# Queues of bulk transfers, split set-up work, and reordered norms in a kernel of two cross-attention layers

## The chip, the cores and the metric

The kernel runs on one core of one Trainium2 chip. The metric is the device time of one execution in microseconds (us), here the median of three runs. A core has a matrix engine, TensorE (PE in the profile, with its weight loads as PEld), and three engines for element-wise work: VectorE (DVE), ScalarE (ACT) and GpSimd (POOL). SyncE (SP) issues transfers between memory and the core; ACT can issue them too, in order with its own computations. Every engine works through its own instructions in order and waits for the others by semaphores.

## The reference

2048 tokens of width 512 (32 sequences of 64) pass through four blocks, each with a residual. `ctx` has the same shape and is the source of keys and values. Masks and shapes apart:

```
x = x + attention0(layernorm(x), ctx, ctx, mask)   # 32 query heads, 8 key heads, rope on q and k
x = x + ffn(layernorm(x))       # silu(h Wg) * (h Wu), then Wd; 4-bit weights, unpacked as
                                # sc[g_idx] * (nibble - (zero[g_idx] + 1))
x = x + attention1(layernorm(x), ctx, mask)        # RMS norm on q and k, with weights
h = layernorm(x);  x = x + h + gate(h) * aux(h)    # aux: 8 slots chosen of 128, softmax over them
```

and the last block, cut to what the change touches:

```
def _L1_ffn_ref(hidden_states, ...):
    ...
    top_scores, top_idx = jax.lax.top_k(router_scores, K)
    ...
    w = jax.nn.softmax(attn, axis=-1)        # over the 8 slots chosen of 128
    sel_vals = aux_values[top_idx]
    aux_out = jnp.einsum('bsk,bskh->bsh', w, sel_vals)
    aux_out = aux_out @ Wvd.T @ Wvu.T
    ...
    gate = jax.nn.sigmoid(gate_w1 * u_norm + gate_bias)
    gate = jnp.where(gate < EARLY_EXIT, 0.0, gate)
    return hidden_states + gate[..., None] * aux_out
```

## The kernel before

The tokens stand in four chunks of 512 (`c` = 0 to 3); `x_sb[c]`, the transposed normalised `xnT[c]` and the transposed `ctxT[c]` stay in on-chip memory throughout. `norm_stats` takes mean and variance on DVE and the inverse root on POOL; `norm_apply` normalises four tiles on DVE (`xna`, `xnb`, `xnc`, `xnd` for the four norms, L167), transposes them on PE (`xta` to `xtd`, L172) and copies them with ACT into `xnT` (L175).

Attention runs over 8 key heads `g` times 4 chunks `c`, 32 steps. `project` makes the four query heads of a group (`pq`), keys and values (`pv`, or `pkv` in layer 1), with the rope on DVE and its last addition on POOL (`qT`, `kT`, L299); in layer 1 `kn` and `pk` are the normalised keys. `scores` makes `S`, `softmax` the probabilities `s`, `values` the product `po` and, by ACT copies, `oT` (L476), and `output` adds `pout` to `x_sb` (L486, L493). In `Attention.run` the order by hand is: the hooks of the step, loads of the next group, values of the step before, scores, output of the step before, softmax, and projection of the next step. A scheduler orders what is free to move by the data it needs; the order within an engine is fixed when the program is built.

The feed-forward block runs over 6 groups of 256 inner columns times 4 chunks: `ffn_load` fetches the 4-bit weights, `ffn_dequant` unpacks them with DVE, using products of PE (`pgz`, `pdz`) of the one-hot group index `oh` with scales and zero points `sz`; `ffn_up` makes `pgu`, `ffn_down` `pd`. `sz` and `oh` are made once by `ffn_constants`: six scale pieces for gate and up and one for down (`scales_gu`, `scales_down`), two zero-point pieces (`qz`, unpacked into `zi`), and four group-index pieces (`g_idx_gu`, `g_idx_down`), each fetched into a temporary tile, of which there are two, shared with the rope. The whole function is the hook of step (1,0).

The last block: `mem_constants` loads and folds its weights (hook of layer 1's step (1,0)); per chunk `mem_weights` makes router scores and takes the best 8, `mem_softmax` is a softmax over 128 slots for each of four token tiles, `mem_values` transposes the weights (`pwt`, copied to `wT`) and multiplies with the folded values (`paux`), `mem_gate` makes the gates, and `mem_out` adds and stores.

Transfers before: on SP's queue the weights of each group and `x` of chunks 1 to 3; on ACT's queue the first `x`, `ctxT`, `cosT`, `sinT`, the masks (`mraw`, `mask0`), the norm weights `q_norm` and `k_norm`, and all of `ffn_constants` and `mem_constants`.

Of the kernel before, what the change touches and what calls it, by code (L numbers as in the profile page):

```python
# [18 lines left out]
P = 128  # L19
# [23 lines left out]
def tile_xattn_ffn_2_layers(ctx: ExitStack, tc: tile.TileContext, a: dict, out: bass.AP):  # L43
# [19 lines left out]
    def m2_tile(name):  # L63
        return ap_.tile([P, CH], F32, tag="m2", name=name, bufs=4)
# [55 lines left out]
    def load_mask(c):  # L120
        w = NH * KH * S
        mraw[c] = m2_tile(f"mraw{c}")
        nc.scalar.dma_start(mraw[c][:, 0:w], a["mask1"][:, c * w : (c + 1) * w])

    def mask_flags(c):
        w = NH * KH * S
# [72 lines left out]
    class Attention:  # L199
# [31 lines left out]

        def load_out(self, g):
            w = w8_tile(f"wo{self.L}_{g}")
            nc.sync.dma_start(
                w,
                a[self.names[3]][g * GQ * HD : (g + 1) * GQ * HD, :].rearrange(
                    "(h p) n -> p h n", p=P
                ),
            )
            self.wo[g] = w  # L240

        def project(self, g, c):
            return self.project0(g, c) if self.L == 0 else self.project1(g, c)
# [251 lines left out]
        def start(self):  # L495
            self.state = self.project(0, 0)

        def run(self, hooks, joined, after, between=lambda c: None):

            steps = [(g, c) for g in range(NKV) for c in range(NCH)]
            state = self.state
            before = None
            for i, (g, c) in enumerate(steps):
                for hook in hooks.get((g, c), ()):
                    hook()
                if c == 0 and g + 1 < NKV:
                    self.load_in(g + 1)
                if c == NCH - 1 and g + 1 < NKV:  # L510
                    self.load_out(g + 1)
                if before is not None:
                    oT = self.values(*before)
                st, rb = self.scores(g, c, state)
                if g == NKV - 1 and c > 1:
                    between(c - 2)
                if before is not None:
                    self.output(*before[:2], oT)
                probs = self.softmax(g, c, st, rb)
                done = before is not None and before[0] == NKV - 1  # L520
                if done:
                    joined(before[1])
                if i + 1 < len(steps):
                    nxt = self.project(*steps[i + 1])
                if done:
                    after(before[1])
                before, state = (g, c, state, probs), nxt
            oT = self.values(*before)
            between(NCH - 2)
            self.output(*before[:2], oT)  # L530
            joined(before[1])
# [5 lines left out]
    ffn = {}  # L537

    def ffn_constants():

        sz = const.tile([P, 2 * INTER], BF16, tag="sz", name="sz")
        oh = const.tile([P, INTER], BF16, tag="oh", name="oh")
# [16 lines left out]
        for base, cnt, name in ((R_GS, NG, "scales_gu"), (R_DS, NGD, "scales_down")):  # L559
# [3 lines left out]
            for at in range(0, total, CH):  # L563
                w = min(CH, total - at)
                s = tmp_tile(f"{name}{at}")
                v, part = s[rows, 0, 0:w], s[:, 1, :].bitcast(BF16)[rows, 0:w]
                for k in range(3):
                    nc.scalar.dma_start(
                        s[base + k * cnt : base + (k + 1) * cnt, 0, 0:w], a[name][:, at : at + w]
                    )  # L570
                for by in (p1, p2):
                    nc.vector.tensor_copy(part, v)
                    nc.vector.scalar_tensor_tensor(v, part, by, v, ALU.mult, ALU.add)
                nc.vector.tensor_copy(sz[rows, at : at + w], v)
        qz = m2_tile("qz").bitcast(U32)
        zi = m2_tile("zi").bitcast(U32)
        for base, cnt, name in ((R_GZ, NG, "qzeros_gu"), (R_DZ, NGD, "qzeros_down")):
            w = a[name].shape[1]
            rows = slice(base, base + cnt)
            nc.scalar.dma_start(qz[rows, 0:w], a[name])  # L580
            zv = sz[rows, 0 : 8 * w].rearrange("p (w e) -> p w e", e=8)
            for e in range(8):
                nc.vector.tensor_scalar(
# [5 lines left out]
                    ALU.bitwise_and,  # L589
                )  # L590
                nc.vector.tensor_copy(zv[:, :, e], zi[rows, 0:w])
        for base, cnt, parts, name in (
            (R_GS, NG, 3, "g_idx_gu"),
            (R_GZ, NG, 1, "g_idx_gu"),
# [5 lines left out]
            for at in range(0, total, CH):  # L600
                w = min(CH, total - at)
                gt = tmp_tile(f"{name}{base}_{at}")
                gv, o = gt[rows, 0, 0:w].bitcast(I32), gt[rows, 1, 0:w]
                nc.scalar.dma_start(
                    gv, a[name][0:1, at : at + w].to_broadcast([parts * cnt, w])
                )

# [3 lines left out]
                nc.vector.tensor_scalar(  # L611
                    oh[rows, at : at + w], o, pidx[rows, 0:1], None, ALU.is_equal
                )
        ffn["sz"], ffn["oh"] = sz, oh

    groups = [(f, min(FG, INTER - f)) for f in range(0, INTER, FG)]
# [86 lines left out]
    def ffn_down(i, c, hT):  # L703
        tiles = ffn_tiles(i)
        for tk in range(TT):
# [8 lines left out]
                )  # L714
            nc.vector.tensor_tensor(x_sb[c][:, tk, :], x_sb[c][:, tk, :], p, ALU.add)

    def ffn_run(hooks, joined, last):


# [6 lines left out]
                joined(pending[1])  # L726

        for i, c in steps:
            hT = ffn_up(i, c)
            for hook in hooks.get((i, c), ()):  # L730
                hook()
            if pending is not None:
# [9 lines left out]

    mem = {}

    def mem_constants():
        fc = const.tile([P, KT * (BOT + P) + D + 3 * NSLOT + 5], F32, tag="fc", name="fc")
        tp = a8_tile("memtmp").rearrange("p a b -> p (a b)")
        at = [0, 0]
# [4 lines left out]
            at[which] += width  # L753
            return s

        q = nc.scalar
        mem["wq"] = carve(0, P, KT * BOT).rearrange("p (k n) -> p k n", k=KT)
        mem["wu1"] = carve(0, P, KT * P).rearrange("p (k n) -> p k n", k=KT)
        mem["v3"] = carve(0, P, D)
# [12 lines left out]
        q.dma_start(mem["wq"], a["WqT"].rearrange("(k p) n -> p k n", p=P))  # L772
        q.dma_start(mem["wu1"], a["Wu1T"].rearrange("(k p) n -> p k n", p=P))
        q.dma_start(mem["lr"], a["log_rel"].to_broadcast([P, NSLOT]))
        q.dma_start(mem["wu2"], a["Wu2T"])
        q.dma_start(mem["bu1"], a["bu1"])
        q.dma_start(mem["gw"], a["gate_w1"].to_broadcast([P, 1]))
        q.dma_start(mem["gb"], a["gate_bias"].to_broadcast([P, 1]))
        q.dma_start(mem["bu2"], a["bu2"].to_broadcast([P, 1]))
        q.dma_start(keys, a["keysT"])  # L780
        q.dma_start(wr, a["Wr"])
        q.dma_start(wrT, a["WrT"])
        q.dma_start(valT, a["valuesT"].rearrange("(k p) n -> p k n", p=P))
        q.dma_start(wvd, a["WvdT"].rearrange("(k p) n -> p k n", p=P))
        q.dma_start(wvu, a["WvuT"])

        p = mm_tile("prk")
        nc.tensor.matmul(p[0:RDIM, 0:NSLOT], wrT, keys, start=True, stop=True)
# [14 lines left out]
        nc.vector.tensor_copy(mem["v3"], p)  # L803
        mem["vst"] = const.tile([P, NT, 2], F32, tag="vst", name="vst")
        mem["lrn"] = const.tile([P, NT], F32, tag="lrn", name="lrn")

    def mem_each(c, t, xn):

# [55 lines left out]
    def mem_softmax(c, behind=None):  # L864
        if behind is not None:
            with tc.issue_after(behind):
                return mem_softmax(c)
        att, bc = mem["att", c], [P, TT, NSLOT]
        mx = sm.tile([P, TT], F32, tag="mx", name=f"mmx{c}")
        sums = sm.tile([P, TT], F32, tag="sums", name=f"msum{c}")  # L870
# [76 lines left out]
    att0, att1 = Attention(0), Attention(1)  # L947
    last = NCH - 1
    att0.load_kv(0)
    att0.load_q(0)  # L950
    load_ctx(0, nc.scalar)
    nc.scalar.dma_start(cosT, a["cosT"])
    nc.scalar.dma_start(sinT, a["sinT"])
    load_mask(0)
    for c in range(1, NCH):
        load_x(c, nc.sync)
        load_ctx(c, nc.scalar)
        if c == 1:
            att0.load_out(0)
    for j in range(4):  # L960
        nc.scalar.dma_start(mask0[j * KB : (j + 1) * KB], a["mask0"])
# [7 lines left out]
    def behind_first(c):  # L969
        with tc.issue_after(first):  # L970
# [120 lines left out]
```

## Time and profile before

| | |
|---|---|
| three runs | 3195.83, 3197.95, 3198.1 us; median 3197.95 |
| profiled execution | 3197.32 us; its span 3195.5 us, mean granted clock 0.98 |
| idle before the first transpose of PE | 11.9 us |
| largest waits of PE after that | 15.5 (`pq`), 9.7 (`pwt`), 7.6 (`pk`) us |
| PE's time in `pout`, `pq` of layer 0, `pq` of layer 1 | 901.0, 447.0, 451.1 us |
| one step of layer 0's attention | about 38.5 us |
| moved bytes | 67.13 MB, mean 21 GB/s |

The granted clock is the share of full speed at which PE was allowed to run. Times within the execution count from the start of its span. A wait is written as: who waited, for which tile, then who released it.

### The profile page before, as it was taken

How to read it: one execution, taken by the hardware profiler on the slowest of the kernel's cores; microseconds unless marked ns; L12 is line 12 of the kernel's file. 1: busy time of each engine (PE TensorE's matmuls, PEld its weight loads, DVE VectorE, ACT ScalarE, POOL GpSimd, SP SyncE). 2: the span in 40 equal slices, each digit the busy share in tenths (PEclk: the TensorE clock that was granted, in tenths of full speed). 3: DMA queues.
4: the chain of work that ended last, by engine and by line, in shares of the span. 5: the costliest groups of instructions: out<-in, count | busy, mean ns of one | idle time of the engine just before them, and what ended most of it. 6: DMA issues, size and time to landing. Idle time of an engine off the chain costs nothing. (4 is left out here: it accounts for less than half of the span.)

```text
span 3195.5 us, 30089 instructions
## 1 busy us (share of the span) xinstructions
PE 3094.4 (97%) x12454; PEld 1590.4 (50%) x12454; DVE 1466.0 (46%) x2384; ACT 503.7 (16%) x917; POOL 609.1 (19%) x464
## 2 busy tenths in 40 slices
PE   6999999999999999999999999999999999999987
PEld 3545555555555555444444455555555555555443
DVE  6586555554555556323222443343443433333455
ACT  0100000001101001100000122222222222222222
POOL 2212222222222222000000022222222222222221
PEclk8999999999999999999999999999999999999998
DMA  5010101010000000000000000000000000100001
GB/s 173 5 36 1 34 1 34 0 34 19 15 20 14 20 14 20 13 20 20 5 20 16 20 7 26 14 20 14 20 14 20 14 25 10 33 1 14 1 1 53
DMA packets 54159, 67.13 MB, mean 21 GB/s; under 512 B 6229, under 2 KB 29901, under 8 KB 54023
## 3 DMA queue, kind: packets, MB, share of 16 engines
q1 hardware_dynamic: 46284, 57.75, 5.5%
q10 hardware_dynamic: 7739, 7.47, 0.7%
q8 instruction: 98, 1.61, 0.2%
q14 instruction: 38, 0.31, 0.0%
HBM read 61.01 MB, written 4.19 MB: 20 GB/s over the span
## 5 line engine op out<-in xcount | busy, mean ns | idle before, releaser
L486 PE MATMUL pout<-wo,oT 128*128 128x512 f32 x2048 | 901.0, 598 | 6.9 <-ACT oT L476 6.9
L486 PEld LDWEIGHTS pout<-wo,oT 128*128 128x128 f32 x2048 | 385.5, 191 | 496.0 <-issue 462.3
L276 PE MATMUL pq<-xnT,wq 128*128 128x512 f32 x1024 | 447.0, 595 | 15.5 <-ACT xnT L175 15.5
L340 PE MATMUL pq<-xnT,wq 128*128 128x512 f32 x1024 | 451.1, 593 | 0.0
L276 PEld LDWEIGHTS pq<-xnT,wq 128*128 128x128 f32 x1024 | 195.3, 191 | 261.5 <-issue 245.1
L691 PE MATMUL pgu<-xnT,wgu 128*128 128x512 f32 (+1 forms) x704 | 315.4, 606 | 0.3 <-DVE wgu L649 0.2
L340 PEld LDWEIGHTS pq<-xnT,wq 128*128 128x128 f32 x1024 | 192.6, 191 | 216.6 <-issue 214.7
L449 POOL TENSOR_TENSOR s<-s,ib 128x512 f32<-128x512 f32 x128 | 160.6, 1276 | 677.8 <-DVE ib L190 669.3
L493 DVE TENSOR_TENSOR x<-x,pout 128x512 f32<-128x512 f32 x256 | 169.3, 670 | 140.6 <-PE pout L486 140.5
L316 PE MATMUL pkv<-wkv,ctxT 128*128 128x256 f32 x1024 | 226.6, 379 | 0.4 <-DVE x L493 0.4
L691 PEld LDWEIGHTS pgu<-xnT,wgu 128*128 128x128 f32 (+1 forms) x704 | 134.9, 192 | 177.4 <-issue 171.4
L316 PEld LDWEIGHTS pkv<-wkv,ctxT 128*128 128x128 f32 x1024 | 194.6, 190 | 40.3 <-issue 13.8
L299 POOL TENSOR_TENSOR qT<-rope 128x512 f32<-128x512 f32 x128 | 162.1, 1267 | 263.9 <-DVE rope L298 260.6
L296 DVE TENSOR_TENSOR rope<-pq,cosT 128x512 f32<-128x512 f32 x160 | 110.5, 691 | 222.1 <-PE pq L276 141.3
L145 POOL TENSOR_TENSOR qr<-qs,nhalf 128x16 f32<-128x16 f32 x32 | 92.8, 2901 | 446.8 <-DVE qs L375 446.8
L356 DVE TRANSPOSE_TENSOR_REDUCE part<-q 128x16 f32<-128x512 f32 x128 | 90.7, 708 | 174.2 <-ACT q L353 169.9
L263 ACT COPY v<-pv 128x512 f32<-128x512 f32 x32 | 18.8, 588 | 872.3 <-PE pv L256 838.8
L708 PE MATMUL pd<-wd,hT 128*128 128x512 f32 (+1 forms) x352 | 155.0, 592 | 0.0
L476 ACT COPY oT<-po 128x512 f32<-128x512 f32 x256 | 131.7, 599 | 104.4 <-PE po L468 99.9
L468 PE MATMUL po<-s,v 32*128 32x256 f32 x2048 | 140.6, 396 | 5.3 <-DVE rope L298 4.3
L444 ACT ACTIVATE s<-s 128x1024 f32<-128x1024 f32 x64 | 67.6, 1057 | 473.1 <-DVE s L442 473.1
L700 DVE TENSOR_TENSOR hT<-hT,pgu 128x512 f32<-128x512 f32 (+1 forms) x44 | 30.2, 687 | 240.9 <-PE pgu L691 240.9
(205 smaller groups left out, 2631.4 us busy)
## 6 DMA issues: line engine op xcount, KB each, us to landing
wq<-in_L_wq SPq DMA_DIRECT2D x8, 1024.0 KB
wo<-in_L_wo SPq DMA_DIRECT2D x8, 1024.0 KB
wq<-in_L_wqT SPq DMA_DIRECT2D x8, 1024.0 KB
wo<-in_L_woT SPq DMA_DIRECT2D x8, 1024.0 KB
wgu<-in_qweight_gu SPq DMA_DIRECT2D x40, 128.0 KB
ctxT<-in_ctxT ACTq DMA_DIRECT2D x4, 1024.0 KB
out<-o SPq DMA_DIRECT2D x16, 256.0 KB
x<-in_x SPq DMA_DIRECT2D x12, 256.0 KB
```

The costliest lines, as they stand in the source:

```text
L276: nc.tensor.matmul(ps, lhsT, rhs, start=(k == 0), stop=(k == KT - 1))
L296: nc.vector.tensor_tensor(t3[:, 0], ps3, over(cosT, 0, HD), ALU.mult)
L299: nc.gpsimd.tensor_tensor(dst, t3[:, 0], t3[:, 1], ALU.add)
L316: nc.tensor.matmul(ps[:, t], ctxT[c][:, k, tok : tok + P], wkv[:, k], start=(k == 0), stop=(k == KT - 1),)
L340: nc.tensor.matmul(ps, wq[:, k, j * HD : (j + 1) * HD], xnT[c][:, k, :], start=(k == 0), stop=(k == KT - 1),)
L449: nc.gpsimd.tensor_tensor(sv[:, f], sv[:, f], ib[:, f * W : (f + 1) * W].unsqueeze(1).to_broadcast([P, KH, W]), ALU.mult,)
L468: nc.tensor.matmul(po[j][:, f * W : (f + 1) * W], v[rows, f, e], probs[rows, f, e], start=(e == 0), stop=(e == KH - 1),)
L476: ins = nc.scalar.copy(o5[:, j], po[j].rearrange("p (f h q) -> p f h q", f=NH, h=GQ))
L486: nc.tensor.matmul(ps, oT[:, h, t * P : (t + 1) * P], self.wo[g][:, h, :], start=(h == 0), stop=(h == GQ - 1),)
L493: nc.vector.tensor_tensor(x_sb[c][:, t, :], x_sb[c][:, t, :], ps, ALU.add)
L691: nc.tensor.matmul(p[0:w_, :], w[:, k, j, t * P : t * P + w_], xnT[c][:, k, :], start=(k == 0), stop=(k == KT - 1),)
L708: nc.tensor.matmul(p, hT[0:w_, t, tk * P : (tk + 1) * P], wd[i][0:w_, t, :], start=(t == 0), stop=(t == len(tiles) - 1),)
```

## The change

Five things change.

The transfers of `ctxT`, `cosT`, `sinT`, the masks, the norm weights, the feed-forward constants and the last block's constants are issued by SP; ACT issues the first `x` alone. Their order at the start becomes: keys and values, `ctx` 0, queries, `cos`, `sin`, mask 0, `x` 1, `ctx` 1, output weight, then `x` and `ctx` of chunks 2 and 3, `mask0`, norm weights.

`ffn_constants` becomes a generator of 13 pieces, and each step of the groups 1 to 6 runs the next one, until there are none.

The first `ffn_up` is placed behind the last projection of layer 0's attention (`tail`), ahead of that attention's last `norm_apply` calls; the last chunk's norm moves from the hook of (0,0) to that of (0,1); and layer 1's first projection is placed ahead of the norm of chunk 2.

`mem_constants` is placed behind the load of an output weight of layer 1.

`mem_softmax` takes the negated maximum as the bias of one exponential for each token tile, whose running sum is kept (`mem["sums"]`); the weights are no longer divided by their sum, and `mem_out` divides the gate by it.

```diff
-        nc.scalar.dma_start(mraw[c][:, 0:w], a["mask1"][:, c * w : (c + 1) * w])
+        nc.sync.dma_start(mraw[c][:, 0:w], a["mask1"][:, c * w : (c + 1) * w])
...
-            nc.sync.dma_start(
+            ins = nc.sync.dma_start(
...
             self.wo[g] = w
+            self.loaded = ins.ins
...
                     nxt = self.project(*steps[i + 1])
+                else:
+                    tail()
...
                 for k in range(3):
-                    nc.scalar.dma_start(
+                    nc.sync.dma_start(
...
                 nc.vector.tensor_copy(sz[rows, at : at + w], v)
+                yield
...
-            nc.scalar.dma_start(qz[rows, 0:w], a[name])
+            nc.sync.dma_start(qz[rows, 0:w], a[name])
...
                 nc.vector.tensor_copy(zv[:, :, e], zi[rows, 0:w])
+            yield
...
-                nc.scalar.dma_start(
+                nc.sync.dma_start(
                     gv, a[name][0:1, at : at + w].to_broadcast([parts * cnt, w])
...
+            yield
         ffn["sz"], ffn["oh"] = sz, oh
...
+    def ffn_first():
+        ffn["first"] = ffn_up(0, 0)
...
-            hT = ffn_up(i, c)
+            hT = ffn_up(i, c) if (i, c) != (0, 0) else ffn["first"]
...
-    def mem_constants():
+    def mem_constants(behind):
...
-        q = nc.scalar
+        q = nc.sync
...
+        with tc.issue_after(behind):
+            q.dma_start(mem["wq"], a["WqT"].rearrange("(k p) n -> p k n", p=P))
...
         nc.vector.tensor_reduce(mx, att, AX.X, ALU.max)
-        nc.vector.tensor_tensor(att, att, mx.unsqueeze(2).to_broadcast(bc), ALU.subtract)
-        nc.scalar.activation(att, att, AF.Exp)
-        nc.vector.tensor_reduce(sums, att, AX.X, ALU.add)
-        nc.vector.reciprocal(sums, sums)
-        nc.vector.tensor_tensor(att, att, sums.unsqueeze(2).to_broadcast(bc), ALU.mult)
+        nc.vector.tensor_scalar(mx, mx, -1.0, None, ALU.mult)
+        for t in range(TT):
+            nc.scalar.activation(
+                att[:, t, :], att[:, t, :], AF.Exp, bias=mx[:, t : t + 1],
+                accum_out=mem["sums"][:, c * TT + t : c * TT + t + 1],
+            )
...
         gate = mem["gate", name]
+        sums = mem["sums"][:, c0 * TT : c1 * TT]
+        nc.vector.reciprocal(sums, sums)
+        nc.vector.tensor_tensor(gate, gate, sums, ALU.mult)
...
     att0.load_kv(0)
+    load_ctx(0, nc.sync)
     att0.load_q(0)
-    load_ctx(0, nc.scalar)
-    nc.scalar.dma_start(cosT, a["cosT"])
-    nc.scalar.dma_start(sinT, a["sinT"])
+    nc.sync.dma_start(cosT, a["cosT"])
+    nc.sync.dma_start(sinT, a["sinT"])
     load_mask(0)
-    for c in range(1, NCH):
+    load_x(1, nc.sync)
+    load_ctx(1, nc.sync)
+    att0.load_out(0)
+    for c in range(2, NCH):
         load_x(c, nc.sync)
-        load_ctx(c, nc.scalar)
-        if c == 1:
-            att0.load_out(0)
+        load_ctx(c, nc.sync)
     for j in range(4):
-        nc.scalar.dma_start(mask0[j * KB : (j + 1) * KB], a["mask0"])
-    nc.scalar.dma_start(wqk[:, 0:1], a["q_norm"])
-    nc.scalar.dma_start(wqk[:, 1:2], a["k_norm"])
+        nc.sync.dma_start(mask0[j * KB : (j + 1) * KB], a["mask0"])
+    nc.sync.dma_start(wqk[:, 0:1], a["q_norm"])
+    nc.sync.dma_start(wqk[:, 1:2], a["k_norm"])
...
+    pieces = ffn_constants()
...
-            (1, 0): [ffn_constants],
+            **{
+                (g, c): [lambda: next(pieces, None)] for g in range(1, NKV - 1) for c in range(NCH)
+            },
...
+        tail=ffn_first,
...
-            (0, 0): [lambda: norm_apply(last, "b")],
+            (0, 1): [lambda: norm_apply(last, "b")],
...
-        lambda: (norm_apply(last - 1, "c"), att1.start()),
+        lambda: (att1.start(), norm_apply(last - 1, "c")),
...
-        {(0, 1): [lambda: norm_apply(last, "c")], (1, 0): [mem_constants]},
+        {(0, 1): [lambda: norm_apply(last, "c")], (1, 0): [lambda: mem_constants(att1.loaded)]},
```

In the built program the pieces end up thus on DVE: a scale piece stands between the last rope and the predicated copy of its step; both zero-point pieces stand together ahead of the ropes of step (2,3); the sixteen small operations of `pidx` (L555 to L558) stand ahead of the first `xna`, where seven of them stood behind the third.

More of the change, by code (lines that the diff above doesn't have):

```diff
@@ L496, in start, with run @@
             self.state = self.project(0, 0)
-        def run(self, hooks, joined, after, between=lambda c: None):
+        def run(self, hooks, joined, after, between=lambda c: None, tail=lambda: None):
             steps = [(g, c) for g in range(NKV) for c in range(NCH)]
@@ L771, in mem_constants @@
         v2 = carve(1, VB, NSLOT)
[L772 to L785, printed above, removed]
+        with tc.issue_after(behind):
+            q.dma_start(mem["wq"], a["WqT"].rearrange("(k p) n -> p k n", p=P))
+            q.dma_start(mem["wu1"], a["Wu1T"].rearrange("(k p) n -> p k n", p=P))
+            q.dma_start(mem["lr"], a["log_rel"].to_broadcast([P, NSLOT]))
+            q.dma_start(mem["wu2"], a["Wu2T"])
+            q.dma_start(mem["bu1"], a["bu1"])
+            q.dma_start(mem["gw"], a["gate_w1"].to_broadcast([P, 1]))
+            q.dma_start(mem["gb"], a["gate_bias"].to_broadcast([P, 1]))
+            q.dma_start(mem["bu2"], a["bu2"].to_broadcast([P, 1]))
+            q.dma_start(keys, a["keysT"])
+            q.dma_start(wr, a["Wr"])
+            q.dma_start(wrT, a["WrT"])
+            q.dma_start(valT, a["valuesT"].rearrange("(k p) n -> p k n", p=P))
+            q.dma_start(wvd, a["WvdT"].rearrange("(k p) n -> p k n", p=P))
+            q.dma_start(wvu, a["WvuT"])
         p = mm_tile("prk")
@@ L805, in mem_constants @@
         mem["lrn"] = const.tile([P, NT], F32, tag="lrn", name="lrn")
+        mem["sums"] = const.tile([P, NT], F32, tag="msums", name="msums")
     def mem_each(c, t, xn):
@@ L867, in mem_softmax @@
                 return mem_softmax(c)
-        att, bc = mem["att", c], [P, TT, NSLOT]
+        att = mem["att", c]
         mx = sm.tile([P, TT], F32, tag="mx", name=f"mmx{c}")
-        sums = sm.tile([P, TT], F32, tag="sums", name=f"msum{c}")
         nc.vector.tensor_reduce(mx, att, AX.X, ALU.max)
-        nc.vector.tensor_tensor(att, att, mx.unsqueeze(2).to_broadcast(bc), ALU.subtract)
-        nc.scalar.activation(att, att, AF.Exp)
-        nc.vector.tensor_reduce(sums, att, AX.X, ALU.add)
-        nc.vector.reciprocal(sums, sums)
-        nc.vector.tensor_tensor(att, att, sums.unsqueeze(2).to_broadcast(bc), ALU.mult)
+        nc.vector.tensor_scalar(mx, mx, -1.0, None, ALU.mult)
[4 more added lines that the diff above has]
+            )
     def mem_values(c):
```

## The prediction

> **What bounds the kernel now.** I read the engines' shares first, then TensorE's waits, then the timeline around each wait, and last the windows for the clock. The shares and the slices:
>
> ```profile
> PE 3094.4 (97%) x12454; PEld 1590.4 (50%) x12454; DVE 1466.0 (46%) x2384; ACT 503.7 (16%) x917; POOL 609.1 (19%) x464
> PE   6999999999999999999999999999999999999987
> ```
>
> TensorE (PE) is the bound from the second slice on, and the change takes no matmul away. So it can win only PE's idle time, 3195.5 - 3094.4 = 101.1 us, and busy time spent at a lowered clock. Any cost on DVE, ACT, POOL or a queue counts only if PE waits for it. PE's waits (who waited <- who released: sum, times, longest):
>
> ```profile
> PE pq L276 <- ACT xnT L175: 15.5, 1, 15.5
> PE pout L486 <- ACT oT L476: 6.9, 4, 3.3
> PE xtc L172 <- DVE xnc L167: 4.9, 1, 4.9
> PE po L468 <- DVE rope L298: 4.3, 3, 1.9
> PE xtb L172 <- DVE xnb L167: 3.8, 1, 3.8
> ```
>
> The two largest waits besides, 11.9 us before the first transpose and 9.7 us before the last `pwt`, sit at the start and the end. The timeline tells why the first wait above exists (start, duration, engine or issue queue, count, idle time before and its releaser):
>
> ```profile
> 23.63 7.90 ACTq L961 DMA_DIRECT2D mask<-in_mask  x4
> 34.38 1.28 ACT L175 ACT_TABLE_LOAD   x1 [34.38 <-DMA mask<-in_mask]
> 37.78 2.93 PE L276 MATMUL pq<-xnT,wq 128*128 128x512 f32 x3 [15.48 <-ACT xnT L175]
> ```
>
> ACT's own queue was issuing transfers until 34.38 and only then copied `xnT`, although the transposes were there at about 14. Windows (busy of PE, PEld, DVE, ACT, POOL, then PE's granted clock, DMA share, GB/s):
>
> ```profile
> 24.00:26.00 2.00, 0.00 (x0) 0.00 (x0) 1.51 (x4) 0.00 (x0) 0.00 (x0) 0.79 1.04 385
> 42.00:54.00 12.00, 12.00 (x30) 5.29 (x29) 6.38 (x10) 0.00 (x0) 4.73 (x4) 0.99 0.00 0
> 250.00:262.00 12.00, 10.10 (x30) 5.74 (x29) 10.37 (x15) 1.66 (x3) 6.00 (x5) 0.57 0.00 0
> 480.00:560.00 80.00, 80.00 (x344) 40.95 (x343) 41.20 (x60) 7.39 (x12) 18.89 (x15) 1.00 0.10 34
> ```
>
> The reader is to see that transfers run at 385 GB/s early on, that a stall also halves the clock for a time after (0.57 around 256; the clock falls in multiples of 3.41 us), and that in the steady part PE is full while DVE idles half of the time.
>
> **The start.** The mask and norm-weight loads, `ctx`, `cos`, `sin` and mask pieces leave ACT's queue; ACT keeps the first `x` and then copies. The wait of 15.48 goes. PE's granted clock was 0.5 from 25.1 to 42.2; of that, 4.2 us of busy time would have taken 2.1. Against it, sixteen small `pidx` operations now all stand before the first `xna` on DVE, where seven stood after the third: at some 0.15-0.17 us each (`DVE L556 TENSOR_SCALAR pidx` took 0.15) that makes 2.65 us later for the first transpose, all of it exposed. The last `pq` group ends at 53.80 - 15.48 - 2.1 + 2.65 = 38.9, a gain of 14.9. Does SP's single queue keep up? Ahead of `pq` stand `wk`, `wv`, `ctx0`, `wq0` beside `x0`: 3.7 MB; the first 10 us moved 2.8 MB (282 GB/s), the rest at 385 GB/s is there at 12.3, and `pq` wants it at 25. `x2`, whose statistics stand between two ropes on DVE, is there after 8.3 MB, at 24.3, and the rope behind it is wanted at 28.5. So nothing waits, with 4 us to spare at the tightest place.
> What is late next: S(0,0) needs the last rope and its POOL addition, 3.8 us behind the last `pq` (57.56 - 53.80). Before, PE filled 2.8 us of that with sixteen transposes and one first product. After, `xna` of chunk 1 stands behind that rope on DVE and only one transpose group (0.5) fits: 2.3 us lost. Such a pause (3.3 us) is the size of the one that ended at 208.79 (3.26 us), after which the clock was 0.5 for 3.41 us, 1.7 us of work: I take 1.6. Start: 14.9 - 2.3 - 1.6 = **11.0** (9 to 13). The 0.91 us gap before `po` at 82.22 (released by a rope of DVE, which has chunk 2's statistics behind it by then) I count as gone: **0.9** (0 to 0.9).
>
> **Constants in pieces.** Before, one hook at step (1,0) put all 13 groups into the queues: their issues stood on ACT's queue and their conversions on DVE. Between 202 and 255 PE paused 1.41, 3.26, 0.82, 1.52 and 1.90 us, 8.9 in all:
>
> ```profile
> 249.53 2.94 PE L468 MATMUL po<-s,v 32*128 32x256 f32 x8 [1.52 <-DVE rope L298]
> 254.38 2.08 PE L468 MATMUL po<-s,v 32*128 32x256 f32 x8 [1.90 <-DVE rope L298]
> ```
>
> and ran at half clock for 3.4 us from 209.5 and 10.2 us from 250.4, busy 3.4 and 8.3 of them: 11.7 x 1/2 = 5.9. Here a rule and the row part. The Trainium skill, "TensorE: Matmul & The Clock Gate" (section "Why this matters for your kernels"), says that the clock falls after an idle pause of more than about 3 us between bursts. By it only the 3.26 us pause costs clock, the pauses of 0.8 to 1.9 us cost none, and the stretch is worth 8.9 + 1.7 = 10.6. The row shows 0.57 in a window whose longest pause is 1.90, so I count 8.9 + 5.9 = 14.8.
> In the changed kernel a scale piece is five DVE operations (0.41 + 0.73 + 0.41 + 0.73 + 0.40 = 2.7 us) in a step that has 38.5 us, of which DVE is busy 41.2 / 80 = half; it stands between the last rope and the predicated copy, where DVE idles 5.2 us in every step. Hidden. The two zero-point groups did not separate: their 32 operations (8 x (0.33 + 0.95 + 0.19 + 0.31) = 14.2 us, some 17 with the gaps) stand together ahead of the ropes of step (2,3), as they stood before ahead of those of (1,0), where S paused 1.41. That pause I keep, with 0.9 of its kind behind it. Each later `g_idx` piece of twelve operations is 6 us, 1 to 3 over its cover, but the probabilities are ready some 23 us before `po` wants them. So 14.8 - 2.3 = **12.5**; ends 9 (the rule) and 14.8.
> SP's queue: a piece's DMA waits in order behind a weight load that waits for its buffer. A load of 1 MB takes 2.7 us at 385 GB/s and is wanted about three steps (115 us) later. Cost 0. If the cover is gone, the piece stands in front of DVE's next ropes: see the third rival.
>
> **Norms behind first products.** At the end of layer 0 the wait of 3.76 before `xtb` gets 13.9 us of first `pgu` products ahead of it: 3.76, and the clock window at 0.5 from 1298.3 (3.41, busy) 1.7: **5.5** (3.8 to 6). The half clock from 1264.2 to 1281.2 comes from dequantisation among S and `pgz`, which no edit moves: 0. Before the second attention the wait of 4.94 before `xtc` gets `pkv` and `pq` ahead (14 us): 4.94, and of the 0.5 window from 1806.9 (6.8 us, busy 3.7) 1.8: **6.7** (5 to 7). The 7.61 pause before `pk` waits for `kn`, whose copies stand behind an exponential on ACT; it stays, ends -3 to +3.
>
> **Slot sums from the exponential.** Per chunk DVE loses a subtraction (0.69), a reduction (0.68), a reciprocal (0.18) and a product (0.87), 2.4 us, and gains a negation (0.16). ACT's one exponential over 512 columns (0.63) becomes four over 128 with a sum. From rows: an exponential over 12 columns took 0.21, so one over 128 is 0.21 + 116 x 0.42/500 = 0.31, four 1.2. The skill, "ScalarE: Activation LUTs" (section "Rules for kernel authors"), speaks against the split: about 0.3 us for every ACTIVATE and 0.83 ns a column, thus 4 x 0.41 = 1.6 against 0.73. By row ACT loses 0.6, by rule 0.9; the sum's own cost shows in no row (0 to 0.2 each). DVE's chain is 2.2 shorter against it, so the chain wins 1.0 to 1.6 at each use. In the last steps the two pauses of 1.6 before `paux` shorten to about 0.7, the one of 0.39 goes and that of 3.22 shortens by about 1: **3.0**. At the end DVE runs without a break from 3170 to 3192: less 2.4, plus 0.16, plus two reciprocals and products on small tiles (4 x about 0.2) is 1.4; the output transfers, 4.2 MB from 3180.17 on, need 10.9 of the 11.9 us in which they are issued, so I take **1.3**. The 14 loads of the last layer's constants on SP are wanted over 1000 us later or once at `prk`: 0.
>
> **The sum.** 11.0 + 0.9 + 12.5 + 5.5 + 6.7 + 4.3 = 40.9 us. The profiled execution took 3197.32 (span 3195.5); 3197.3 - 40.9 = 3156.4. The median of the runs shown is 0.6 above the profiled one, so 3157.
>
> **Rivals.**
> 1. *The pauses move instead of going.* The zero points stall PE as 248-256 shows, clock included, and the start waits for `x2` or `mask` behind the 1 MB loads on the one queue. The stretch is then worth 3 and the start 6: 40.9 - 9.5 - 5.0 = 26.4, 3171. For it: 32 DVE operations in one lump, and PE idle after the first heads. Against: 4 us to spare.
> 2. *The clock gives more.* With pauses gone, half-clock windows that I left (17 us from 1264, 6.8 from 1858, 10.2 from 3114, 13.6 from 3175) shrink by half: 24 us at half, up to 12 more and so 3145. Against: their pauses remain.
> 3. *Slower: DVE waits in line for a piece.* Its conversion cannot be passed; behind it are the next ropes, behind these S. DVE can lose about 5.2 us before the copy and 8 before a rope stops PE (17 us of zero points made 1.41), 13 in all. If SP holds back pieces behind a weight load that waits for its buffer, one whole step each (38.5) in the three groups, PE stops 25.5 us times 3 for two pieces each, 153 us: 3197 - 41 + 153 = 3309. It decides, slower than before, from a sum of 41 us past the cover, 3.2 us per piece. Against: the buffer that `wq` waits for comes free within the step before.
> 4. *The table of waits names the wrong releaser at the start*, and `xnT` is late for another reason: without the start 3168, and 3180 if the constants' stretch too is set by DVE work that is all still there.
>
> Chances: forecast 0.60 (3148 to 3166 by the terms' ends), rival 1 0.18, rival 2 0.10, rival 3 0.05, rival 4 0.07. Range 3143 to 3176: it takes in 1, 2 and part of 4. A change below 0.2% (6.4 us) could not be told from none: faster 0.94, same 0.02, slower 0.04.
>
> **What would show it.** First `pq` head at about 25 with no wait; S(0,0) at about 43 with a pause of 3 us before; no pause over 1.5 us between 190 and 260 less 12; one near the zero points, some 7 steps (270 us) later; no wait before `xtb` and `xtc`; the 7.61 still there; `paux` pauses under 1 us. Wrong: DVE waits for piece transfers over 10 us, or clock windows at 0.5 in steady steps.

## The result, and the profile after

The changed kernel takes 3150.97 us (median of four runs, 3147.16 to 3153.53) against 3197.07 us: ratio 0.9855, 95% interval 0.9838 to 0.9872, 46 us less. The profiled execution took 3153.53 us, its span 3151.7 us; it is the longest of the four. The forecast was 3157 us, a gain of 40.9.

The page's first lines (busy time, share of the span, instructions; then the busy tenths in 40 slices):

```profile
span 3151.7 us, 30114 instructions
PE 3081.2 (98%) x12454; PEld 1583.8 (50%) x12454; DVE 1467.0 (47%) x2376; ACT 507.7 (16%) x945; POOL 607.5 (19%) x464
PE   7999999999999999999999989999999999999987
```

PE's idle time fell from 101.1 to 3151.7 - 3081.2 = 70.5 us, and its busy time by 13.2 us with the same 12454 matmuls. So some 30 us of the gain are pauses, and 13 are matmuls that took longer before. PE's waits:

```profile
PE xta L172 <- DVE xna L167: 18.7, 2, 14.7
PE pk L351 <- DVE kn L334: 7.9, 1, 7.9
PE pwt L896 <- ACT xnT L885: 5.8, 1, 5.8
PE pout L487 <- ACT oT L477: 4.1, 3, 2.1
PE paux L901 <- ACT wT L898: 2.8, 4, 0.7
PE S L388 <- POOL qT L300: 1.4, 1, 1.4
```

`pq` on `xnT`, `xtb`, `xtc` and `po` on the rope are gone from the list. New in it is a second `xta` pause; 7.9 before `pk` stayed. The timeline of PE at the start (start, duration, count, then the idle time before and its releaser):

```profile
14.69 3.41 PE L172 MATMUL xta<-ident,xna 128*128 128x128 f32 x16 [14.69 <-DVE xna L167]
24.94 13.90 PE L277 MATMUL pq<-xnT,wq 128*128 128x512 f32 x32
42.81 1.08 PE L172 MATMUL xta<-ident,xna 128*128 128x128 f32 x4 [3.97 <-DVE xna L167]
44.82 2.82 PE L172 MATMUL xta<-ident,xna 128*128 128x128 f32 x12
47.57 2.33 PE L388 MATMUL S<-qT,kT 128*32 128x256 f32 x30
```

and four windows (busy of PE, PEld, DVE, ACT, POOL, granted clock, DMA share, GB/s), to be held against those of before:

```profile
24.00:26.00 2.00, 2.00 (x13) 1.51 (x13) 1.91 (x5) 0.59 (x1) 1.01 (x1) 1.00 1.05 383
42.00:54.00 12.00, 11.19 (x58) 6.33 (x59) 6.74 (x16) 2.34 (x4) 1.40 (x2) 0.73 0.04 12
176.00:256.00 80.00, 80.00 (x344) 40.94 (x343) 48.88 (x69) 7.39 (x12) 18.96 (x16) 1.00 0.05 14
480.00:560.00 80.00, 80.00 (x344) 40.94 (x343) 42.90 (x61) 7.39 (x12) 17.84 (x14) 1.00 0.05 14
```

In 24 to 26, PE now works while the transfers still run at 383 GB/s. From 176 to 256, where the constants' lump used to be, PE is full: DVE carries 48.9 us in 80 instead of the steady 42.9, and no one waits for it.

To see where the 43.8 us between the two spans arose, I took the start of the same matmul in both traces and followed the difference:

| stretch, by the kernel before | gained at its end, in all | in the stretch | forecast |
|---|---|---|---|
| start, to the first `pout` (86) | 9.7 | 9.7 | 11.9 |
| the lump of constants (200 to 268) | 29.4 | 19.7 | 14.8 |
| zero points at step (2,3) | 27.2 | -2.3 | -2.3 |
| end of layer 0 and first `pgu` (to 1347) | 36.7 | 9.6 | 5.5 |
| feed-forward steps (to 1788) | 34.0 | -2.7 | 0 |
| start of layer 1 (to 1878) | 38.9 | 4.9 | 6.7 |
| last steps and end | 43.8 | 4.9 | 4.3 |

The sum came out well, but most of its terms did not. The experiments are about these. A second pair of profiles, of the same two kernels, gave for the same seven stretches 8.9, 21.4, -2.3, 5.3, 0.8, 4.8 and 4.8 (43.6 in all): the first, second, fourth and fifth terms differ from profile to profile by one to four us.

### The profile page after: what moved, and what is told of

Read it like the earlier page. It is cut to its first block, busy times and chain, and to the rows that moved or that the text cites. A ratio compares the mean times of both kernels' runs of the same rounds, so it can differ in the third digit from the quotient of the medians.

```text
span 3151.7 us, 30114 instructions
## 1 busy us (share of the span) xinstructions
PE 3081.2 (98%) x12454; PEld 1583.8 (50%) x12454; DVE 1467.0 (47%) x2376; ACT 507.7 (16%) x945; POOL 607.5 (19%) x464
## 4 chain that ended last, share of the span: by engine, by line
PE 93%; DVE 4%; POOL 1%; ACT 1%; issue 0%; DMA 0%; SPq 0%; ACTq 0%; DVEq 0%; POOLq 0%
PE pout L487 27%; PE pq L277 17%; PE pq L341 14%; PE pgu L698 10%; PE pkv L317 7%; PE pd L715 5%; PE po L469 4%; PE S L388 4%; PE pv L257 3%; PE pqy L831 1%; PE pk L351 0%; PE pu L838 0%; PE xta L172 0%; DVE sz L596 0%; DVE wgu L655 0%
## 5 line engine op out<-in xcount | busy, mean ns | idle before, releaser
L469 PE MATMUL po<-s,v 32*128 32x256 f32 x2048 | 132.2, 391 | 0.1
```

The source lines that it names most:

```text
L469: nc.tensor.matmul(po[j][:, f * W : (f + 1) * W], v[rows, f, e], probs[rows, f, e], start=(e == 0), stop=(e == KH - 1),)
```

## Experiments

Half clock below means a granted clock of 0.5.

Theory: the edits act each in its own place, by the pauses that they take from PE; where a place gained more or less than forecast, the stretches at half clock did it. Rivals: the queue matters and not the splitting; the reordering at the end of layer 0 changes the clock itself; the start is bound by its transfers.

**The start alone.** The kernel before, with the changed order of loads on SP's queue:

```diff
-    load_ctx(0, nc.scalar)
-    nc.scalar.dma_start(cosT, a["cosT"])
+    load_ctx(0, nc.sync)
...
+    nc.sync.dma_start(cosT, a["cosT"])
```

> The kernel before, with the changed kernel's loads at the start alone (order and queue, masks too); the feed-forward constants stay on ACT's queue in one lump at step (1,0). Theory (ACT's own issues held back its copies): the first query head starts at about 25 instead of 37.8, S(0,0) follows a pause of some 4 us, and the first output product starts 9.7 us earlier than before (86.0 - 76.3, as in the changed kernel); then the pauses between 200 and 260 are all there, moved forward by that much, 8.9 us idle. Time about 3187 (3184 to 3190). Rival (the copies were late for another reason, or the gain is given back at the lump): 3194 to 3198.

3186.86 us, ratio 0.9975 (0.9966 to 0.9984), 8.2 less. The timeline of ACT in this run:

```profile
17.16 0.59 ACT L175 COPY xnT<-xta 128x512 f32<-128x512 f32 x1 [2.32 <-PE xta L172]
19.72 0.59 ACT L175 COPY xnT<-xta 128x512 f32<-128x512 f32 x1 [0.27 <-PE xta L172]
```

These are the first and the last of the four copies. ACT now copies as soon as PE has transposed, from 17.16 on instead of 35.67. The first `pout` came 8.16 us earlier than before; the first transpose came at 16.0 here (14.7 in the changed kernel), which is most of the 1.5 us to 9.7. In this run ACT still issued eight loads of the last block's constants ahead of its first copy (2.9 to 13.5 us; before, they stood behind the copies), and the last tile of the first `x` was ready at 10.3 instead of 8.9. Whether the one made the other is not shown: over all the profiles that tile came at 8.9 to 10.4. The lump's pauses were all there (five of over 0.7 us between 190 and 250, 8.4 us in all). The theory holds.

**Pieces, by either queue, and the lump on SP.** Three kernels: before with pieces issued by SP, before with pieces issued by ACT, and the changed kernel with all pieces at once:

```diff
+    pieces = ffn_constants()
...
-            (1, 0): [ffn_constants],
+            **{
+                (g, c): [lambda: next(pieces, None)] for g in range(1, NKV - 1) for c in range(NCH)
+            },
```

```diff
-            **{
-                (g, c): [lambda: next(pieces, None)] for g in range(1, NKV - 1) for c in range(NCH)
-            },
+            (1, 0): [lambda: list(pieces)],
```

> The kernel before, with the constants alone cut in pieces over steps and issued by SP. Theory (a lump on two engines stalled PE, and SP has room for the pieces): start unchanged, 19.7 us gained between the fifth step and the seventh, 2.3 given back where the zero points stand, 17.4 net: 3180 (3177 to 3183). Rival (SP holds pieces back and DVE waits in line): waits of DVE for these transfers over 10 us, less than 10 us gained.

> As the last, but the pieces are issued on ACT's queue as before. If the splitting over steps is what counts, three issues of about 0.3 us in a step don't reach PE: 3180, same as with SP. If the queue counts (an issue that waits for a temporary tile holds ACT's copies of v and oT behind it, 3.3 us as once before), up to 13 steps pause: 13 x 3 = 39 us lost against SP's, about 3219.

> The changed kernel, with all pieces at once at step (1,0), still issued by SP. If DVE's lump sets the pauses: of the 19.7 us the part on DVE's account comes back (pauses before po and its stretched products, 12 us), the part on ACT's (the copies of oT, 7 us) does not: 3151 + 12 - 2 = 3161. If ACT's queue was the whole cause: 3149, with the pause before S near the zero points gone from step (2,3).

Pieces on SP: 3176.49 us, 0.9941 (0.9926 to 0.9956). Pieces on ACT: 3173.40 us, 0.9933 (0.9916 to 0.9949). Past step (2,3) they had gained 17.7 and 17.9 us by the matmuls' starts, with the one pause of 1.42 before S at the zero points in both. So the queue makes no difference once the work is split: the rival that ACT's issues hold back its copies in every step is out. The lump on SP: 3168.90 us, 0.9921 (0.9906 to 0.9936), 18 us slower than the changed kernel, more than expected. PE's timeline there:

```profile
231.04 1.96 PE L469 MATMUL po<-s,v 32*128 32x256 f32 x8 [0.82 <-ACT v L264]
239.42 6.42 PE L469 MATMUL po<-s,v 32*128 32x256 f32 x24 [6.42 <-DVE rope L299]
```

The pause of 3.26 before `pout` is gone, as expected with ACT's queue free, and with its half clock that is 5.0 us. But DVE's ropes stand behind some 60 conversions, in this kernel as in the one before, and here they start 6.1 us after PE's last `pv` product instead of 2.2; so PE pauses 6.42 here. What PE gains on ACT's account it mostly loses again, waiting for DVE. Of before's stretch the lump on SP saves 2.4 net (12.4 gained, 10.0 of it at the start). **The splitting is worth 15 to 18 us, the queue of the constants 2.4 or less.**

The traces also show why I undervalued this term. The same 32 products `po`, first in the kernel before, then with pieces on ACT:

```profile
246.05 1.96 PE L468 MATMUL po<-s,v 32*128 32x256 f32 x8 [0.82 <-ACT v L263]
249.53 2.94 PE L468 MATMUL po<-s,v 32*128 32x256 f32 x8 [1.52 <-DVE rope L298]
254.38 3.79 PE L468 MATMUL po<-s,v 32*128 32x256 f32 x16 [1.90 <-DVE rope L298]
```

```profile
237.46 2.01 PE L468 MATMUL po<-s,v 32*128 32x256 f32 x32
```

1.96 + 2.94 + 3.79 = 8.69 us against 2.01. Half clock makes at most 4.0 of 2.01, so 4.7 us have another cause. The windows show it, again first the kernel before, then pieces on ACT:

```profile
246.50:248.00 1.50, 1.50 (x8) 0.95 (x6) 1.36 (x3) 0.00 (x0) 0.00 (x0) 1.00 0.08 9
```

```profile
237.50:239.00 1.50, 1.50 (x29) 1.44 (x32) 1.43 (x3) 0.58 (x1) 0.01 (x1) 1.00 0.00 0
```

At full clock and with PE busy throughout, 1.5 us hold 8 products in the one and 29 in the other. A product `po` uses 32 rows of the array. With pieces, four of them, one for each quarter of the array's rows, start within 0.02 us of one another, and the next four 0.216 us later. In the kernel before, the first eight of this step start singly at that same pitch of 0.216, the next eight singly too, and the last sixteen in pairs: the groups waited for different operations (the releasers above). PE did not wait inside these records; it ran one or two products where it has room for four. As an estimate from these rows, at full clock the three groups would take 3 x 1.96 = 5.9 us: of the 6.7 lost, 3.9 are the products that no longer ran side by side, and 2.8 are half clock.

**The other edits, each alone.** First `pgu` ahead of the last norms, with the last chunk's norm one step later:

```diff
+                else:
+                    tail()
...
-            (0, 0): [lambda: norm_apply(last, "b")],
+            (0, 1): [lambda: norm_apply(last, "b")],
```

> The kernel before, with the first feed-forward products behind the last projection alone (and the last chunk's norm one step later). Theory: the pause of 3.76 us before xtb goes, and 1.7 us of half clock with it: 5.5 us, 3189.5; the rest of the 9.6 us that the changed kernel gained at this place (half clock for 6.8 instead of 17.1 us) belongs to the clock's windows and may or may not appear. Rival (the reordering shortens the half clock itself): 9 us or more gained here, with a window of 7 us or less at 1264, 3185. Second rival (the later norm of the last chunk costs): the changed kernel's 2.7 us lost in the feed-forward steps appear here too as a pause.

3190.63 us, 0.9984 (0.9976 to 0.9992): 5.0 less, as the theory has it. Half clock stood from 1265.2 to 1282.3, 17.1 us as in the kernel before. One profile cannot settle the rival, since the length varies by itself (see below); all of them do better: at this place the seven profiles with the reordering had 6.8 to 17.1 us of half clock, 11.7 on average, the seven without it 10.2 to 17.1, on average 12.2. So it shortens the half clock little, if at all. In the first layer's steps the trace stood 0.5 to 0.9 us behind before's (its start was later), by the end of the feed-forward steps 5.3 ahead, with values between 3.8 and 6.3 on the way and no pause to show for these: the changed kernel's -2.7 is of this kind.

Layer 1's first projection ahead of a norm:

```diff
-        lambda: (norm_apply(last - 1, "c"), att1.start()),
+        lambda: (att1.start(), norm_apply(last - 1, "c")),
```

> The kernel before, with layer 1's first projection ahead of the norm of chunk 2 alone. Theory: the pause of 4.94 us before xtc goes and nothing else does, since the pause before pk stays and keeps its half clock: 4.9 us, 3190 (the changed kernel gained 4.9 here). If the clock window goes too, 6.7, 3188.5. Rival (the pause moves to pk): pk's pause grows by several us, less than 3 gained.

3191.65 us, 0.9989 (0.9982 to 0.9996), 3.9 less; between the last feed-forward steps and layer 1 the trace gained 4.5. The pause before `xtc` is gone, and what follows is the same as before:

```profile
1853.52 1.09 PE L350 MATMUL pk<-ident,kn 128*128 128x128 f32 x4 [7.87 <-DVE kn L333]
```

7.87 against 7.61. The half clock that I had counted at `xtc` (1.8) did not come off in full: before, two stretches of 6.8 us began at 1806.9 and 1858.1; here, and in the changed kernel, a single one of 10.2 begins in the pause before `pk`.

Slot sums from the exponential:

```diff
-        nc.scalar.activation(att, att, AF.Exp)
-        nc.vector.tensor_reduce(sums, att, AX.X, ALU.add)
...
+        nc.vector.tensor_scalar(mx, mx, -1.0, None, ALU.mult)
+        for t in range(TT):
+            nc.scalar.activation(
+                att[:, t, :], att[:, t, :], AF.Exp, bias=mx[:, t : t + 1],
+                accum_out=mem["sums"][:, c * TT + t : c * TT + t + 1],
+            )
```

> The kernel before, with the slot sums from the exponential alone. Theory: per chunk 1 us less before paux (1.6 to 0.7), 3 to 4 us in the last steps, and at the end 1.3 to 1.6 from DVE's shorter chain: 4.9 as in the changed kernel, 3190. Each exponential of 128 columns 0.4 with 0.19 to read its sum, 1.6 us for four against 0.63. Rival (ACT's longer chain eats it): pauses of paux unchanged, 3194 to 3196.

3190.37 us, 0.9984 (0.9977 to 0.9991), 5.2 less. The timeline of ACT and PE in the changed kernel's end, two of the four exponentials:

```profile
3136.49 0.40 ACT L885 ACTIVATE xnT<-xnT,mmx 128x128 f32<-128x128 f32 x1 [2.15 <-DVE mmx L883]
3136.80 0.19 ACT L885 ACTIVATION_READ_ACCUMULATOR xnT<-xnT,mmx 128x1 f32 x1
3136.89 0.39 ACT L885 ACTIVATE xnT<-xnT,mmx 128x128 f32<-128x128 f32 x1
3137.03 1.63 PE L896 MATMUL pwt<-ident,xnT 128*128 128x128 f32 x4 [5.76 <-ACT xnT L885]
```

One every 0.39 us, 1.65 for four with the reads, against 0.63 for the one before. But the first transpose starts after the first exponential, and DVE's subtraction, sum, reciprocal and product no longer stand ahead of it, so PE pauses 5.76 before `pwt` instead of 9.66 (in this run too). How much either of the two does was not separated.

**Does the half clock belong to the kernel, or to chance?** Both kernels once more, unchanged.

> The changed kernel itself once more, to see what of its profile belongs to the clock. If the half-clock windows near the end of layer 0's attention and in the feed-forward steps belong to the kernel, they stand at the same places with the same lengths (6.8 us at 1240, then 6.8, 6.8, 3.4, 6.8, 3.4), and the gain at each point is the same to 0.1 us. If they belong to where the clock's windows happen to fall, they differ by multiples of 3.41 us, the gains between 1240 and 1690 by about 1.7 us for each, and the idle pauses are the same to 0.1 us.

> The kernel before once more, for the same question: the half clock of 17.1 us at 1264 is there again if the kernel makes it so; if it is the windows' luck, 10.2 or 6.8 us appear as in other profiles in which nothing near this place was changed, and the pauses of PE stay as they were.

3150.32 us, 0.9855 (0.984 to 0.987), and 3196.70 us, 1.0001. PE's pauses were the same to 0.2 us but for the first ones at the start, one before `pout` and one before `po` (0.4 each). The clock was not. The windows view for the end of layer 0, first the changed kernel, then its second profile:

```profile
1232.00:1254.00 22.00, 19.92 (x111) 9.89 (x111) 16.24 (x27) 5.65 (x10) 0.52 (x1) 0.84 0.20 57
```

```profile
1232.00:1254.00 22.00, 20.47 (x108) 10.19 (x108) 15.30 (x24) 5.65 (x10) 1.07 (x1) 0.69 0.22 63
```

and the kernel before, first and second profile:

```profile
1260.00:1282.00 22.00, 20.34 (x96) 8.90 (x95) 14.92 (x24) 5.45 (x10) 0.00 (x0) 0.61 0.17 50
```

```profile
1260.00:1282.00 22.00, 20.31 (x112) 10.09 (x111) 15.05 (x24) 5.65 (x10) 1.02 (x1) 0.77 0.22 62
```

The columns are as above: 0.84 and 0.69, 0.61 and 0.77 for the same program. Half clock here was 6.8 and 13.7 us, and 17.1 and 10.2. At one matmul near 1255 the two profiles of the changed kernel are 3.0 us apart, at 1838 only 0.4. So of the 9.6 us at the end of layer 0, some 5 are a long stretch at half clock in the one profile and a short one in the other; between the second profiles that place gained 5.3, where 5.5 were forecast.

**What the start still loses, and the end.** The changed kernel with the `pidx` operations held behind the first norm; then also with the norm of chunk 1 between the query heads; then also with the last gate and eight of the stores taken forward:

```diff
-        for base, cnt, parts in ((R_GS, NG, 3), (R_GZ, NG, 1), (R_DS, NGD, 3), (R_DZ, NGD, 1)):
...
+        with tc.issue_after(first):
+            for base, cnt, parts in ((R_GS, NG, 3), (R_GZ, NG, 1), (R_DS, NGD, 3), (R_DZ, NGD, 1)):
```

```diff
             for j in (GQ, 0, 1, 2, 3):
+                if j == 2 and first:
+                    behind_start()
...
+    def behind_start():
+        norm_next(0)
```

```diff
-    mem_weights(last, mem_mean)
-    mem_gate("a", 0, last)
...
+    mem_weights(last, lambda: mem_store("a", 0, 0, last - 1), early_gate)
```

> The changed kernel with the small index operations held behind the first norm, nothing else. First transposes at 12.0 to 12.2 instead of 14.7, and all of the 2.5 us kept to the first output product, as nothing waits for another thing there: 3148.5. If the pause before S(0,0) stays at 4 us with its half clock, it is a matter of the order on VectorE and not of when the step begins; the last run's remaining gain at the first output product (4.7 in all) is then 2.2 for the earlier norm of chunk 1.

> The changed kernel, with the small index operations held behind the first norm, and the norm of chunk 1 placed between the first two and the last two query heads of the first step. If these two are what the start still loses: first transposes 2.65 us earlier, the pause of 3.97 us before S(0,0) falls to 1 or less, and its half clock (xta 1.1 + 2.75 instead of 1.75, S 3.25 instead of 1.93, 3.4 us in all) goes: 2.65 + 3 + 3.4 = 9 us, 3142 (3140 to 3146). If the start is bound by its transfers: the first query head waits for xnT or weights instead, 3148 to 3151.

> As e9_norm1, and besides the mean of the last gate is made between the second and third product of the last router query, the gate of chunks 0 to 2 right after it, and the sums and stores of chunks 0 and 1 ahead of the last chunk's router scores. If the end is set by VectorE's unbroken work after the last scores, some 20 small operations and 8 sums (8 x 0.73 = 5.9 us) leave it, and the stores begin 8 us or more earlier: 4 to 6 us less than e9_norm1, 3141. If it is set by the chain from the last scores over paux: 2 us less or nothing, since the sums taken forward push that chain back.

`pidx` alone: first transposes at 12.72, 2.0 us earlier than in the changed kernel, although the first `x` was ready 0.8 later in this profile. The first `pout` came 2.4 us earlier, but only in part by this: the query heads started 1.15 earlier, and the other 1.2 are the half clock behind the pause of 3.97, 3.4 us here and 6.8 there. That pause stayed to the hundredth, so it does not hang on when the step begins but on DVE's order. The time, 3151.93 us, 0.9862 (3147.76 to 3155.23), cannot show 2.4 us. With the norm of chunk 1 forward: 3146.61 us, 0.9842 (0.9826 to 0.9858), first `pout` 4.7 earlier, half of the 9 expected. PE's timeline:

```profile
43.17 1.93 PE L390 MATMUL S<-qT,kT 128*32 128x256 f32 x32 [1.26 <-POOL qT L302]
65.63 0.63 PE L172 MATMUL xta<-ident,xna 128*128 128x128 f32 x4 [1.71 <-DVE xna L167]
66.19 3.63 PE L471 MATMUL po<-s,v 32*128 32x256 f32 x32
```

The pause before S fell to 1.26 as expected, but the last tile of chunk 2's norm is late next (1.71), and the half clock stands there (`po` 3.63 instead of 2.01). With the stores forward: 3148.30 us, 0.9848 (0.9833 to 0.9863), no gain on that. The first store is issued at 3120.91, but

```profile
3135.04 1.63 PE L901 MATMUL pwt<-ident,xnT 128*128 128x128 f32 x4 [10.14 <-ACT xnT L890]
```

the pause before the last `pwt` grew from 5.76 to 10.14: four of the sums taken forward stand on DVE between the operations of the last scores (4 x 0.74 us), and ACT loads its table for the exponentials only when these are due (1.28), since the gate's own exponential now stands earlier. The first store is issued 10.9 us earlier than in the run before, and the end did not move: it is not the stores that end the kernel, but, as this pause has it, the chain over `paux`. The version with `pidx` and the norm of chunk 1 moved has the lowest median, 4 us below the changed kernel; the intervals of the two overlap.

## Why the prediction was right, term by term

**The start** (11.0 and 0.9 forecast, 9.7 measured, 8.9 in the second pair). The last `pq` ended at 38.84, forecast 38.9. From the last statistics of the first `x` to the first `xna`, DVE took 5.1 us with `pidx` ahead and 2.4 without, so `pidx` cost 2.7, forecast 2.65. The step that was mis-sized is what is late next: the pause before S(0,0) with its transposes, 3.97 instead of 3.3. The trace shows what is longer there:

```profile
41.08 1.59 DVE L167 TENSOR_SCALAR xna<-x,mva,rsa 128x512 f32<-128x512 f32 x1
41.12 1.26 POOL L300 TENSOR_TENSOR qT<-rope 128x512 f32<-128x512 f32 x1 [1.70 <-DVE rope L299]
```

This `xna` took 1.59 us instead of 0.54, while POOL made its addition; in both kernels every normalised tile that took over 0.9 us had an addition of POOL beside it, and those with none took 0.50 to 0.55. The half clock behind the pause was 6.8 us (`xta` 1.08 + 2.82, S 2.33, more than usual) instead of one stretch of 3.41; in the second profile of the changed kernel it was 3.4, so this part is chance. In that profile the first products behind the transposes ran slowly for longer instead (the first eight `pq` 4.89 us, 3.60 in the first profile).

**The constants** (14.8 less 2.3 forecast; 19.7 less 2.3 measured). The mechanism was right: five pauses gone, a pause of 1.42 at the zero points, and no wait of PE for a piece. The term that was off is the busy time, 5.9 forecast for half clock, 10.7 measured. The half clock was about as large as forecast (by the rows 1.7 in the first stretch, 2.8 in `po` and 1.2 in the `pout` behind it); what I had left out are products that ran one or two at a time instead of four, some 3.9 us. About 1 us is left unexplained. I had shown the rows myself, eight `po` in 2.94 and eight in 2.08 us, and not held them against a step without a stall, in which 32 take 2.01. The rule that I weighed against it (the Trainium skill, "TensorE: Matmul & The Clock Gate") does not cover this place: the clock fell at 250.4, and the longest of PE's pauses since 209 was 1.52 (1.60 in the second profile, where it fell at 249.9). What PE did there was little, products on 32 of the 128 rows one at a time; that this made the clock fall was not tested. The size that followed from the rule, 10.6, was too low.

**Norms behind first products** (5.5 and 6.7 forecast; 9.6 and 4.9 measured, 5.3 and 4.8 in the second pair). The pauses of 3.76 and 4.94 are gone in full, and 7.61 stayed at 7.85, as forecast. The clock around them is not a property of the edits: alone, they gave 5.0 and 3.9 us by time. Rival 2, more by the clock, is what the first profile showed at layer 0's end, in a stretch that the second profile did not repeat.

**Slot sums** (4.3 forecast, 4.9 measured). Four exponentials took 1.65 us with their reads; the rule of the Trainium skill ("ScalarE: Activation LUTs", "Rules for kernel authors") gave 1.6, my row 1.2 plus up to 0.8 for the sum. The two pauses of 1.6 before `paux` fell to 0.68, forecast 0.7; the one of 3.22 before `xtd` and that of 0.39 stayed, which I had down for 1.4 (in the run with this edit alone the 3.22 fell to 1.65), and one before `xtd` shrank for it (2.01 to 1.22). By the matmuls' starts the last steps gave 3.2 (forecast 3.0) and the end 1.7 (1.3).

**The rivals.** Rival 1 (zero points stall PE with the clock, the start waits for `x2`): the stall was the 2.3 forecast, at full clock, and in the changed kernel nothing but the first `x` kept PE's work waiting for a transfer at the start. Rival 3, the slower one, priced waits of DVE for a piece from 13 us on. Small ones exist in the changed kernel's list of waits:

```profile
DVE scales_gu L576 <- DMA scales_gu<-in_scales_gu: 5.3, 6, 3.8
DVE g_idx_down L614 <- DMA g_idx_down<-in_g_idx_down: 5.2, 4, 3.6
```

The longest is 3.8, under the 5.2 that DVE has free at that place, and PE waited for none. Rival 4 fell with the first experiment.

**The sum.** The five runs with one edit each gave 8.2 + 18.6 + 5.0 + 3.9 + 5.2 = 40.9 us, together 46.1. That this sum equals the forecast is chance: by stretch, I had too much at the start and too little at the constants, and the errors partly cancelled. Whether the edits help each other by 5 us stays open; each of the differences is uncertain by 2 to 5 us. The move of the last block's constants to SP was not run alone; from 1878 to 2983, where they are loaded in the changed kernel, the difference between the two traces stayed at 38.9, so there it neither cost nor gained.

## What to carry to other kernels

A lump of set-up work costs where it stands in line ahead of what the bounding engine waits for: split it over the steps' idle places, and the queue that carries it hardly matters. An engine that computes should not issue more of the start's transfers than its first computation needs: that computation stands behind the issues ahead of it. Price a stall by the same group in a step that has none, not by the idle column alone: busy time does not tell how many products run side by side. And before crediting an edit with a change of clock, profile the same program twice.

## What the runs showed of the hardware

- Four products on 32 rows each take no longer than one: at full clock 1.5 us of busy PE held 29 `po` where four ran side by side and 8 where they came singly, at the same pitch of 0.216 us. Released at different times, 32 of them took 8.69 us instead of 2.01, of which half clock explains at most 2.01 more.
- The same program ran 6.8 and 13.7 us at half clock at one place in two executions (17.1 and 10.2 for the other kernel), always in multiples of 3.41 us. The 3.0 us between the two executions at that place had come down to 0.4 some 580 us later.
- A normalised tile of 128x512 took 0.50 to 0.55 us on DVE with POOL idle, and 0.98 to 1.59 where an addition of POOL ran beside it for 0.7 us or more. Which of the two holds up the other was not tested.
- An exponential with a running sum is two instructions: 0.39 to 0.40 us for 128 columns, and 0.19 to read the sum, which overlap to one every 0.39 us.
